# Score products of 128 weight columns, made as four of 32 columns, in a two-layer graph network

## The chip, the core and the metric

The kernel runs on one core of a Trainium2 chip. The metric is the device time of one execution in microseconds (us); lower is better. Three runs of the kernel before took 2897.25, 2900.75 and 2901.69 us; the median is 2900.75.

## What is computed

There are 64 graphs of 256 nodes with 256 features each, in fp32 throughout. Two layers follow each other. The first is a graph attention layer, applied twice, with a feed-forward part. The second is a relational attention layer, and the change lies there. Its core in the reference is:

```python
q = (src @ Wq + bq).reshape(Bb, Nn, h, dh).transpose(0, 2, 1, 3)
k = (src @ Wk + bk).reshape(Bb, Nn, h, dh).transpose(0, 2, 1, 3)
scores = jnp.einsum('bhid,bhjd->bhij', q, k) / np.sqrt(dh)
attn = jax.nn.softmax(scores, axis=-1)
out = jnp.zeros_like(q)
for r in range(Wv.shape[0]):
    v_r = (src @ Wv[r] + bv[r]).reshape(Bb, Nn, h, dh).transpose(0, 2, 1, 3)
    mask = (adj_matrix == r)[:, None]
    out = out + jnp.einsum('bhij,bhjd->bhid', attn * mask, v_r)
attn_out = out.transpose(0, 2, 1, 3).reshape(Bb, Nn, Dm) @ Wo + bo
x = _ln(src + attn_out, g1, beta1)
ff = jax.nn.gelu(x @ W1 + b1, approximate=False) @ W2 + b2
return _ln(x + ff, g2, beta2)
```

There are 8 heads of 32 features (`dh` = 32). The scores of one head are a product over only 32 features: 256 queries by 256 keys.

## The kernel before

The 64 graphs are worked on as 32 pairs. For each pair the kernel makes queries and keys transposed, that is, with the features on the partitions: in the tile `qk`, four heads of 32 features fill the 128 partitions, and two such halves (`c`) hold the eight heads.

TensorE multiplies a stationary operand, the weights (`lhsT`), by a streamed one (`rhs`). A product needs a weight load (PEld in the profile) and a matmul (PE). The array has 128 rows, over which a product sums, and 128 columns, one for each weight column and so for each partition of the output in PSUM. A product that uses only some rows or columns takes a tile of the array, and products in different tiles can be under way together. The profile gives the tile of a group as rows by columns: `128*32` or `32*128`.

Nearly every product of this kernel goes through `by_strips` (lines 160 to 163), which cuts 128 weight columns into four strips of 32, so four products with tiles of 128 rows by 32 columns stand side by side.

The score products do not. The function `scores(n)` (from line 1021) runs four times for each pair, for two graphs (`b`) and two halves of the heads (`c`). It takes four PSUM banks, one per head, and for two halves of the keys (`jc`) and four heads (`o`) it issues one matmul: the weights are 128 keys of one head (32 rows by 128 columns), the streamed operand is the 256 queries of this head. Head `o` has its 32 rows of the array to itself, so the four heads stand side by side in tiles of 32 rows by 128 columns. That is 8 products in one run of `scores`, and 4 x 32 = 128 runs of it, 1,024 products.

Behind it ScalarE takes the exponential of each bank (line 1038), VectorE masks it with the adjacency (L1042) and adds halves (L1046), and `products(n)` multiplies by the values (L1060) and sums the denominators (L1063), in tiles of 128 rows by 32 columns again. Between runs of `scores`, TensorE does other work in strips: feed-forward products of the same or the next layer (L163), projections, graph attention.

The order of all this is made by a planner in the kernel itself (`run`), when the program is built: each step names its costs, and `took(us)` moves the planned clock of TensorE forward. `scores` books `took(0.97)`. The order that results is fixed engine by engine in the program. The tensors have names in the profile: `ps` is any PSUM bank, `a` the exponentials, `m` the masked ones, `v` the values, `w_L_gnn_w_ff` and `w_L_gnn_W` the weights of the last feed-forward products, `ff` their other operand.

## Time and profile before

| what | value |
|---|---|
| the profiled execution | 2901.78 us |
| its span, first to last instruction | 2900.0 us |
| median of three runs | 2900.75 us |
| mean granted TensorE clock | 0.997 |
| TensorE (PE) busy | 2862.7 us |
| VectorE (DVE) busy | 2636.5 us |
| ScalarE (ACT) busy | 1910.2 us |
| weight loads (PEld) busy | 2038.1 us, beside PE |
| score products (L1029), matmul records | 2,048, busy 147.9 us |
| score products, weight-load records | 2,048, mean 184 ns |

A row of the profile's groups names the line of the kernel, the engine, the operation, the output and its inputs, the tile of the array as rows by columns, the shape of the streamed operand and the number of records. Busy time is the time in which at least one instruction of the group was under way, so the mean length of a matmul (some 400 ns) times its count is more than the busy time: four overlap. The ends of matmuls are modelled; their starts are measured. A waiting engine is idle, and the profile names what ended the wait. "issue" means that nothing which the profile shows was waited for.

In fp32 each matmul instruction shows as two weight loads and two matmuls, so the counts are twice those of the code.

### The profile page before, as it was taken

Reading aid. Unit: us, or ns where it says so; the run is one execution under the profiler, and the core shown is the slowest. Engines: PE = TensorE matmul, PEld = TensorE weight load, DVE = VectorE, ACT = ScalarE, POOL = GpSimd, SP = SyncE. Lnnn points to the kernel's source line nnn. Section 1 sums busy time; section 2 is a strip of 40 time slices with the busy share of each in tenths; the row PEclk is TensorE's granted clock in tenths of the full one; section 3 lists DMA queues with packets and bytes.
Section 4 is the critical chain, followed back from the end, with each engine's and each line's share of the span. In section 5 each row is a group of like instructions: output and inputs, shape, how many; then the busy total and the mean of one; then the engine's idle time right before and its main releaser. Section 6 shows DMA issues by size and latency. Waiting matters only on the chain.

```text
span 2900.0 us, 147819 instructions
## 1 busy us (share of the span) xinstructions
PE 2862.7 (99%) x66066; PEld 2038.1 (70%) x66066; DVE 2636.5 (91%) x5873; ACT 1910.2 (66%) x5171; POOL 285.3 (10%) x518
## 2 busy tenths in 40 slices
PE   8999999999999999999999999999999999999997
PEld 5766677877777676776777776776767776667676
DVE  7889999899999999999999999999999999999886
ACT  5656766656766667766567666677676676666765
POOL 0000010101010101101111100101011101010001
PEclk9999999999999999999999999999999999999999
DMA  6221212222222222222222222222222222221100
GB/s 206 74 68 61 78 61 82 74 79 79 65 68 76 83 80 63 78 72 78 80 76 65 69 76 83 75 75 76 68 78 83 73 69 67 77 75 51 54 3 25
DMA packets 207940, 211.85 MB, mean 73 GB/s; under 512 B 22593, under 2 KB 166337, under 8 KB 207041
## 3 DMA queue, kind: packets, MB, share of 16 engines
q1 hardware_dynamic: 206608, 201.79, 21.9%
q8 instruction: 520, 8.52, 1.2%
q14 instruction: 124, 1.01, 0.1%
q10 hardware_dynamic: 688, 0.53, 0.1%
HBM read 137.51 MB, written 64.73 MB: 70 GB/s over the span
## 4 chain that ended last, share of the span: by engine, by line
PE 93%; DVE 3%; DMA 2%; ACT 1%; issue 0%; SPq 0%; ACTq 0%; DVEq 0%; POOL 0%; POOLq 0%
PE ps L163 79%; PE ps L1060 7%; PE ps L1029 4%; PE ps L1063 2%; DMA yT<-home 0%; DVE ff L912 0%; DVE m L1042 0%; DVE x L739 0%; DMA home<-yb 0%; DMA b_ln<-in_ln 0%; DMA w_L_gnn_w_ff1p<-in_L_gnn_w_ff1pm 0%; DMA xw<-in_L_gnn_a1c 0%; DVE h L1046 0%; DVE x L736 0%; DVE ff L508 0%
## 5 line engine op out<-in xcount | busy, mean ns | idle before, releaser
L163 PE MATMUL ps<-w_L_gnn_w_ff,ff 128*32 128x128 f32 x14336 | 423.8, 273 | 2.5 <-DVE ff L508 1.6
L163 PE MATMUL ps<-w_L_gnn_W,ff 128*32 128x128 f32 x14336 | 424.2, 273 | 0.6 <-ACT a L1038 0.4
L163 PEld LDWEIGHTS ps<-w_L_gnn_w_ff,ff 128*32 128x32 f32 x14336 | 397.0, 110 | 35.2 <-issue 8.6
L163 PEld LDWEIGHTS ps<-w_L_gnn_W,ff 128*32 128x32 f32 x14336 | 393.5, 110 | 37.5 <-issue 15.9
L1038 ACT ACTIVATE a<-ps 128x512 f32<-128x512 f32 x512 | 264.3, 602 | 191.2 <-PE ps L1029 184.8
L912 DVE TENSOR_TENSOR ff<-ff 128x1024 f32<-128x1024 f32 x256 | 311.6, 1217 | 55.6 <-PE ps L163 39.7
L730 POOL TENSOR_SCALAR rstd<-squares 128x2 f32<-128x2 f32 x256 | 78.9, 308 | 2587.1 <-ACT unread L725 2586.6
L1042 DVE TENSOR_TENSOR m<-a,adj 128x1024 f32<-128x1024 f32 x256 | 308.1, 1217 | 3.3 <-ACT a L1038 2.9
L163 PE MATMUL ps<-yT,w_L_gnn_W1p 128*32 128x256 f32 x5120 | 305.8, 380 | 3.2 <-DMA yT<-home 3.1
L163 PE MATMUL ps<-yT,w_L_gnn_w_ff1p 128*32 128x256 f32 x5120 | 306.4, 379 | 0.0
L837 ACT ACTIVATE ff<-ps 128x512 f32<-128x512 f32 x384 | 221.1, 588 | 126.8 <-PE ps L163 126.1
L725 ACT ACTIVATE unread<-x,less 128x256 f32<-128x256 f32 x512 | 259.4, 507 | 68.3 <-DVE less L700 53.0
L508 DVE TENSOR_TENSOR ff<-ps,ff 128x512 f32<-128x512 f32 x384 | 255.9, 682 | 36.5 <-PE ps L163 23.3
L999 ACT ACTIVATE qk<-ps,bqk 128x256 f32<-128x256 f32 x256 | 109.7, 470 | 223.4 <-PE ps L163 223.1
L163 PE MATMUL ps<-xw,e 128*32 128x256 f32 (+1 forms) x4032 | 245.5, 383 | 1.3 <-ACT xw L630 1.3
L163 PEld LDWEIGHTS ps<-yT,w_L_gnn_W1p 128*32 128x32 f32 x5120 | 165.7, 110 | 106.0 <-ACT ff L837 6.8
L163 PEld LDWEIGHTS ps<-yT,w_L_gnn_w_ff1p 128*32 128x32 f32 x5120 | 168.7, 110 | 99.0 <-ACT unread L725 0.3
L736 DVE SCALAR_TENSOR_TENSOR x<-x,less,b_ln 128x256 f32<-128x256 f32 x512 | 227.5, 478 | 7.3 <-ACT unread L725 6.6
L739 DVE SCALAR_TENSOR_TENSOR x<-x,rstd,b_ln 128x256 f32<-128x256 f32 x512 | 229.4, 479 | 1.3 <-POOL rstd L731 1.3
L909 DVE TENSOR_TENSOR x<-ps,x 128x256 f32<-128x256 f32 (+1 forms) x384 | 193.9, 505 | 21.4 <-PE ps L163 16.2
L731 POOL TENSOR_TENSOR rstd<-rstd,mhalf 128x2 f32<-128x2 f32 x256 | 205.7, 803 | 21.3
L163 PEld LDWEIGHTS ps<-xw,e 128*32 128x32 f32 x4032 | 135.3, 111 | 84.8 <-issue 2.6
(141 smaller groups left out, 5015.6 us busy)
## 6 DMA issues: line engine op xcount, KB each, us to landing
home<-yb SPq DMA_DIRECT2D x182, 256.0 KB, 2.2
yT<-home SPq DMA_DIRECT2D x728, 64.0 KB, 2.1
rows<-row SPq DMA_DIRECT2D x60, 512.0 KB, 3.9
x<-in_x SPq DMA_DIRECT2D x32, 512.0 KB, 3.8
out<-x SPq DMA_DIRECT2D x64, 256.0 KB, 3.1
input<-in_xT SPq DMA_DIRECT2D x30, 512.0 KB, 3.9
input<-in_adjT SPq DMA_DIRECT2D x29, 512.0 KB, 4.0
m<-in_adjT SPq DMA_DIRECT2D x3, 512.0 KB, 8.8
```

Of the source, the lines that this page charges most:

```text
L163: nc.tensor.matmul(to[at:at + DH], lhsT=lhsT[:, at:at + DH], rhs=rhs, **flags)
L508: nc.vector.tensor_tensor(self.target(*where), self.bank["z"], self.target(*where), ALU.add)
L725: nc.scalar.activation(unread, rows[j], AF.Square, bias=of["less"][:, j:j + 1], accum_out=squares[:, j:j + 1])
L731: nc.gpsimd.tensor_tensor(rstd, rstd, mhalf[:, :2], ALU.pow)
L736: nc.vector.scalar_tensor_tensor(rows[j], rows[j], of["less"][:, j:j + 1], g, op0=ALU.add, op1=ALU.mult)
L739: nc.vector.scalar_tensor_tensor(rows[j], rows[j], rstd[:, j:j + 1], beta, op0=ALU.mult, op1=ALU.add)
L837: return put("scalar", 0.5, lambda: nc.scalar.activation(target(c, h), of, AF.Copy), event, rank=rank_of["copies"])
L909: return put("vector", us, lambda: nc.vector.tensor_tensor(to, of, to, ALU.add), *events, rank=rank_of["last"], frees=frees)
L912: return put("vector", 1.14, lambda: nc.vector.tensor_tensor(to, a, b, op), *events, rank=rank_of["sums"])
L1038: nc.scalar.activation(a[n][q][:, k], ps[2 * q + k], AF.Exp)
L1042: nc.vector.tensor_tensor(m[n][q], a[n][q], adj, ALU.mult)
L1060: nc.tensor.matmul(po[o * DH:(o + 1) * DH, :N], lhsT=v[:, b, jc, at:at + DH], rhs=e[o // 2][:, o % 2, jc * N:(jc + 1) * N], start=r == jc ...
```

## The change

The inner product of `scores` is made in four parts. Each part takes 32 of the 128 weight columns (keys) and writes 32 of the 128 partitions of the same bank. The streamed operand, the 256 queries of the head, is the same for the four parts. The tile becomes 32 rows by 32 columns. A run of `scores` issues 32 products where it issued 8; the planner still books 0.97 us for it.

```diff
     HQ = P // DH
+    PART = 32
     SCALE = 1.0 / math.sqrt(DH)
...
                 at = b * N + jc * P
                 for o in range(HQ):
                     rows = slice(o * DH, (o + 1) * DH)
-                    nc.tensor.matmul(ps[o][:, jc * N:(jc + 1) * N], lhsT=qk[rows, 1, c, at:at + P],
-                                     rhs=qk[rows, 0, c, b * N:(b + 1) * N], start=True, stop=True)
+                    for part in range(0, P, PART):
+                        nc.tensor.matmul(ps[o][part:part + PART, jc * N:(jc + 1) * N],
+                                         lhsT=qk[rows, 1, c, at + part:at + part + PART],
+                                         rhs=qk[rows, 0, c, b * N:(b + 1) * N], start=True, stop=True)
             there = took(0.97)
```

## The prediction

> **What bounds the kernel now.** I read the page first: busy shares, then the chain that ended last.

> ```profile
> span 2900.0 us, 147819 instructions
> PE 2862.7 (99%) x66066; PEld 2038.1 (70%) x66066; DVE 2636.5 (91%) x5873; ACT 1910.2 (66%) x5171; POOL 285.3 (10%) x518
> ...
> PE 93%; DVE 3%; DMA 2%; ACT 1%; issue 0%; SPq 0%; ACTq 0%; DVEq 0%; POOL 0%; POOLq 0%
> PE ps L163 79%; PE ps L1060 7%; PE ps L1029 4%; PE ps L1063 2%; DMA yT<-home 0%; DVE ff L912 0%; DVE m L1042 0%; DVE x L739 0%; DMA home<-yb 0%; DMA b_ln<-in_ln 0%; DMA w_L_gnn_w_ff1p<-in_L_gnn_w_ff1pm 0%; DMA xw<-in_L_gnn_a1c 0%; DVE h L1046 0%; DVE x L736 0%; DVE ff L508 0%
> ```

> TensorE is the bound from end to end, so what the score products (L1029) take on it counts nearly one for one. A busy PE need not be an efficient one, so next the groups of instructions by shape. The columns after the bar are the busy time of the group and the mean ns of one record.

> ```profile
> L163 PE MATMUL ps<-w_L_gnn_w_ff,ff 128*32 128x128 f32 x14336 | 423.8, 273 | 2.5 <-DVE ff L508 1.6 <-DVE ff L912 0.9
> ...
> L1029 PE MATMUL ps<-qk 32*128 32x256 f32 x2048 | 147.9, 400 | 0.0
> L1060 PE MATMUL ps<-m,v 128*32 128x256 f32 x2048 | 135.4, 380 | 0.0
> ```

> A matmul instruction leaves two records in fp32: 1,024 score products show as 2,048. Scores cost 147.9/2048 = 72 ns a record; the weighted products of L1060, which stream the same 256 columns through tiles of 128 rows by 32 columns, 66 ns. Then the one line, and one block of it (16 records) with its neighbours in the timeline.

> ```profile
> L1029 PEld LDWEIGHTS ps<-qk x2048: 181/184/185, 153.2 to 2827.2; 32*128 32x128 f32 x187
> L1029 PE MATMUL ps<-qk x2048: 374/374/478, 153.2 to 2827.4; 32*128 32x256 f32 x187
> ```

> ```profile
> 402.58 1.93 PE L163 MATMUL ps<-w_L_gnn_W,ff 128*32 128x128 f32 x64
> 404.44 1.15 PE L1029 MATMUL ps<-qk 32*128 32x256 f32 x16
> 405.52 1.95 PE L163 MATMUL ps<-w_L_gnn_W,ff 128*32 128x128 f32 x64
> 407.29 1.05 PE L163 MATMUL ps<-yT,w_L_gnn_W1p 128*32 128x256 f32 x16
> 408.15 1.05 PE L1060 MATMUL ps<-a,v 128*32 128x256 f32 x16
> 409.02 1.05 PE L1060 MATMUL ps<-m,v 128*32 128x256 f32 x16
> ```

> From start to start, 16 records of strips of 256 columns take 0.87 us (408.15 to 409.02), which is 54 ns each or four side by side every 0.216 us. The score block takes 1.08 us (404.44 to 405.52): 0.21 more inside itself. The 64 records ahead of it take 1.86, the same 64 behind it 1.77: another 0.09 to 0.11 at the entry, where the shape of the tiles changes. Where the 0.21 lies is seen when another block, at 153.17, is cut into short stretches (of each engine, the x counts the instructions that touch the stretch):

> ```profile
> 153.16:153.19 0.03, 0.03 (x4) 0.03 (x4) 1.00 0.00 0
> 153.19:153.27 0.07, 0.07 (x4) 0.07 (x4) 1.00 0.00 0
> 153.27:153.30 0.03, 0.03 (x4) 0.03 (x8) 1.00 0.00 0
> 153.30:153.49 0.18, 0.18 (x4) 0.18 (x8) 1.00 0.00 0
> 153.49:153.51 0.03, 0.03 (x8) 0.02 (x4) 1.00 0.00 0
> ...
> 153.91:153.94 0.03, 0.03 (x8) 0.00 (x0) 1.00 0.00 0
> 153.94:154.24 0.29, 0.29 (x8) 0.00 (x0) 1.00 0.21 83
> ```

> Four heads start within 0.03 us, a second wave of four at 153.49, the last at 153.91, the next shape at 154.24. So: first wave 0.32, two waves of 0.21, last 0.33, where a hidden wave is 0.216. The first is about 0.10 longer (its weights load in the open: the longest record is 478 against 374 ns, 104 more), the last about 0.11 [...]. Entry, first wave and exit add up to some 0.32 us a block; there are 128 blocks (four for each of 32 pairs), 41 us in all. That is all the change can touch.

> [...] The trace shows the four heads within 0.03 us, some 7 ns apart, for a tile that has two loads and two multiplies. [...]

> **The change, part by part.** The order of instructions is the same on every engine; on PE each row of 8 score products becomes 32, because the planner still books 0.97 us for the block. No wait, buffer or DMA is added; the waits for the four banks stay on the first product of each head.

> 1. Array work: the same. Eight products of 32 rows by 128 columns are half an array-load twice over; 32 of 32 by 32 are 16 tiles, each used twice. If the 16 run together, each tile streams 2 products x 2 passes = 4 waves of 0.216, as before. Cost 0.
> 2. Removed: most of the open first load. With 32 columns the same start in strips shows 24 ns (the shape of 128x128 goes from 273 to 297-298 in its first wave), against 104. Gain 0.08 us a block.
> 3. Added: the sixteenth tile starts later than the fourth. At 6.7 ns a tile, 15 x 6.7 = 0.10 against 3 x 6.7 = 0.02[...]. Loss 0.08 us.
> 4. Drains at entry and exit: still a change of shape, 128 rows against 32. Cost 0. If the smaller tile empties faster [...], gain up to 0.21 us; I take 0.
> 5. Issue: 48 more records a block, each a load and a multiply. No row prices this. From below: 0[...]. From above: at the start of the program, in products of four streamed columns, 8 matmuls touch the first stretch below and 20 the next, so 12 begin within 0.18 us, 15 ns each; with no queue at all the 64th comes at 0.96 us, where the last of the block starts at 0.77 now. Loss at most 0.19 us. I take 0[...].

> ```profile
> 12.30:12.36 0.06, 0.06 (x8) 0.05 (x4) 0.00 (x0) 0.00 (x0) 1.00 1.19 359
> 12.36:12.54 0.18, 0.18 (x20) 0.18 (x12) 0.00 (x0) 0.00 (x0) 1.00 1.10 347
> ```

> 6. Weight loads of tiles on the same rows: strips show four columns loading together. If with row tiling they took turns, [...] (loss of the 0.08 of step 2). I take 0.
> 7. Who reads: ACT's exponentials (L1038) waited 184.8 us for these products, but ACT is 66% busy and off the chain; a shift under 0.1 us is hidden there. A shift of 1 us would hold up PE anyway, through PE's own time.

> Sum of steps 2 and 3: 128 x (-0.08 + 0.08) = 0. On the profiled execution (2901.78 us, of which 2900.0 are span and 1.8 around it) that is 2901.8; the median of the runs shown is 1.0 lower, so I forecast 2901. A difference under 0.2%, 6 us, can't be told from none.

> **The rivals.**
> - *Four lanes, not sixteen* (slower). The trace shows four tiles at once, never more: four row groups or four column groups. If what lets a second tile pass the waiting second pass of a first is a lane per row group or per column group, the four parts of a head (or the four heads of a part) stand in one line: the second pass of a part runs beside the first pass of the next only. A lane then holds 8 products: 9 waves, not 4, so +5 x 0.216 = 1.08 us, less 0.08: +1.0 us x 128 = +128, 3029 us. It decides as soon as the lane is a group and not a tile. For it: no sight of sixteen in fp32. Against: [...] that strips share rows and heads share columns, yet both run four wide.
> - *Issue or loads show* (slower). Steps 5 and 6 at their ends: +0.08 to +0.27 us, +10 to +35: 2911 to 2936. For it: four times the instructions in the same time. Against: the four-column stretch.
> - *Faster*: the drain shrinks with the tile, or first passes are issued before the waiting second ones, halving the skew (-0.05). From -0.05 to -0.29 us (0.08 of load plus 0.21 of drain): -6 to -37, likely near the small end, 2890 us. [...] Against: the drain at the entry is that of the strips, and stays.

> **How the numbers follow.** No change (within 6 us) 0.34; issue or loads 0.24; four lanes 0.15; faster 0.27. The likeliest is no change, 2901, with its own range 2895 to 2907. The range over cases reaches from 2876 (most of faster) to 2936 (issue and loads at their ends) and leaves out the four lanes and the far end of faster, under 0.2 together. Faster by over 0.2%: 0.27; within: 0.34; slower: 0.24 + 0.15 = 0.39.

> **What would show it.** Right: 8,192 score records (4 x 2,048) whose starts come sixteen within about 0.1 us; weight loads near 110 ns; the block still near 1.08 us and 16 or more multiplies touching one short stretch. Step 2 wrong: the longest score matmul stays 100 ns above the median. Step 3 wrong: sixteen starts in much less or more than 0.1. Step 5: gaps between starts with no tile busy, or "issue" ahead of the loads of the next shape. Lanes: never more than four starts per 0.216 us, the block near 2 us, and L1029's share of the chain near doubled. The forecast falls if the block's length moves by more than 45 ns, which is 6 us over 128 blocks.

## The result, and the profile after

The changed kernel took 2952.6 us (median of six runs, 2948.21 to 2954.33) against 2901.22 before (six runs beside them). The ratio is 1.0175, with a 95% interval of 1.0164 to 1.0186: slower by 51 us. The forecast was 2901, with a range up to 2936.

The profiled execution took 2948.21 us, the lowest of the six, with a span of 2946.4: 46.4 more than the span before. TensorE is the bound as before. First the page's span, busy shares and chain by line of the changed kernel, then its groups by shape (busy us and mean ns after the bar), then the one line (durations as min/median/max ns).

```profile
span 2946.4 us, 160107 instructions
...
PE 2911.1 (99%) x72210; PEld 2111.9 (72%) x72210; DVE 2640.9 (90%) x5873; ACT 1909.5 (65%) x5171; POOL 290.6 (10%) x518
...
PE ps L164 78%; PE ps L1063 7%; PE ps L1031 6%; PE ps L1066 2%; DMA x<-in_x 1%; DMA home<-yb 1%; DMA yT<-home 0%; SPq L784 0%; DVE ff L913 0%; PE ps L804 0%; DVE x L740 0%; DVE x L737 0%; ACT unread L726 0%; PE ps L1179 0%; DVE yb L773 0%
```

```profile
L1031 PE MATMUL ps<-qk 32*32 32x256 f32 x8192 | 195.3, 385 | 0.9 <-DVE x L910 0.9
```

```profile
L1031 PEld LDWEIGHTS ps<-qk x8192: 101/104/106, 153.1 to 2875.4; 32*32 32x32 f32 x200
L1031 PE MATMUL ps<-qk x8192: 371/374/399, 153.1 to 2875.7; 32*32 32x256 f32 x200
```

The scores' share of the chain went from 4% to 6%, their busy time from 147.9 to 195.3 us: 47.4 more, about as much as the span grew. VectorE and ScalarE are busy about as long as before (2640.9 and 1909.5 us, against 2636.5 and 1910.2). The open load did shrink: the longest matmul stands 25 ns above the median (399 against 374), where it was 104 before. A weight load takes 104 ns, against 184 before.

The timeline around the same block as before gives its length:

```profile
405.47 1.93 PE L164 MATMUL ps<-w_L_gnn_W,ff 128*32 128x128 f32 x64
407.33 1.61 PE L1031 MATMUL ps<-qk 32*32 32x256 f32 x64
408.88 1.95 PE L164 MATMUL ps<-w_L_gnn_W,ff 128*32 128x128 f32 x64
```

The entry is as before (1.86 us for the 64 records ahead). This block is 1.55 us from its start to the next. Most are shorter: the median of the 128 is 1.425 us, against 1.076 before. The one at 1737.51 is such a block, and its stretches show what happened. The columns are PE and PEld (busy, and the instructions that touch the stretch), then the granted clock and the DMA traffic. Times in the text below count from the start of the block.

```profile
1737.50:1737.60 0.10, 0.10 (x14) 0.10 (x25) 1.00 0.84 328
1737.60:1737.63 0.03, 0.03 (x16) 0.03 (x30) 1.00 1.22 478
...
1737.74:1737.87 0.13, 0.13 (x32) 0.11 (x2) 1.00 0.93 347
1737.87:1737.95 0.08, 0.08 (x32) 0.00 (x0) 1.00 0.98 384
1737.95:1738.06 0.11, 0.11 (x25) 0.10 (x1) 1.00 1.10 428
1738.07:1738.14 0.07, 0.07 (x17) 0.00 (x0) 1.00 0.75 293
1738.14:1738.42 0.28, 0.28 (x31) 0.27 (x30) 1.00 0.13 44
```

Sixteen matmuls begin in the first 0.12 us and are under way together (x16): sixteen tiles do run side by side. By 0.36 us all 32 of the first half of the keys have begun (x32). (A fp32 product leaves two matmul records here, 8,192 for 4,096 products; the text calls them its first and second pass.) Then one product of the second half gets in: its second load is the one near 0.46 us, and x17 later is the sixteen second passes and this product. From 0.57 to 0.63 us no load is under way at all. The 17th product's load began with its tile's second pass (0.241 and 0.240); on the other fifteen tiles the second passes have begun by 0.36, and no load has followed. Only from 0.65 us on do the others follow, and slowly: the next fifteen are spread over 0.23 us, 16.7 ns each, where the first fourteen came 6.7 ns apart.

The starts of the single records add up the lost time of this block. The 18th product begins at 0.650 us. It could have begun at 0.462, one step of 6.7 ns after the 17th (0.456): 0.188 lost. The sixteenth tile's second product comes 0.233 after that, at 16.7 ns a product, and not 0.093 at 6.7: 0.140. Its load is open again: 0.022. The sum is 0.350. The last start of a block moved from 0.771 before to 1.121 us, as much. Times 128 blocks this is 45 us, of the 46.4 in the span.

### The profile page after: what moved, and what is told of

Read it like the earlier page. It is cut to its first block, busy times and chain, and to the rows that moved or that the text cites. A ratio compares the mean times of both kernels' runs of the same rounds, so it can differ in the third digit from the quotient of the medians.

```text
span 2946.4 us, 160107 instructions
## 1 busy us (share of the span) xinstructions
PE 2911.1 (99%) x72210; PEld 2111.9 (72%) x72210; DVE 2640.9 (90%) x5873; ACT 1909.5 (65%) x5171; POOL 290.6 (10%) x518
## 4 chain that ended last, share of the span: by engine, by line
PE 94%; DMA 2%; DVE 2%; ACT 1%; issue 1%; SPq 0%; DVEq 0%; POOL 0%; POOLq 0%; ACTq 0%
PE ps L164 78%; PE ps L1063 7%; PE ps L1031 6%; PE ps L1066 2%; DMA x<-in_x 1%; DMA home<-yb 1%; DMA yT<-home 0%; SPq L784 0%; DVE ff L913 0%; PE ps L804 0%; DVE x L740 0%; DVE x L737 0%; ACT unread L726 0%; PE ps L1179 0%; DVE yb L773 0%
## 5 line engine op out<-in xcount | busy, mean ns | idle before, releaser
L731 POOL TENSOR_SCALAR rstd<-squares 128x2 f32<-128x2 f32 x256 | 86.6, 338 | 2628.1 <-ACT unread L726 2627.5
L164 PEld LDWEIGHTS ps<-yT,w_L_gnn_w_ff1p 128*32 128x32 f32 x5120 | 180.9, 110 | 90.0 <-ACT unread L726 0.4
L164 PEld LDWEIGHTS ps<-xw,e 128*32 128x32 f32 x4032 | 144.3, 111 | 77.1 <-issue 3.3
```

The source lines that it names most:

```text
L164: nc.tensor.matmul(to[at:at + DH], lhsT=lhsT[:, at:at + DH], rhs=rhs, **flags)
```

## Experiments

### Two parts of 64 columns

```diff
-    PART = 32
+    PART = 64
```

> The four parts of 32 columns become two of 64 (tiles of 32 rows by 64 columns, 16 products a block). Theory W, a window in the matrix engine: it holds some 64 to 68 instructions that are issued and not finished, let go in order; a product in fp32 is 4 of them, so the 18th product of the changed block waits for the first tile's second pass (0.46 to 0.65 us after the block's start). With 16 products the block is 64 instructions and fits: no gap, an open load of about 0.05 us, eight tiles 0.05 us apart from first to last, block about 1.05 us, 2896 to 2902 us. Theory R, a rule of the tile: a second product in a tile of less than 128 columns holds back all others until it is under way. Then a gap of about 0.19 us stays, block about 1.25 us, about 2922 us.

Measured: 2900.22 us, ratio to the kernel before 0.9999 (0.9991 to 1.0007). The line and one block in the timeline:

```profile
L1031 PE MATMUL ps<-qk x4096: 371/374/426, 152.3 to 2827.2; 32*64 32x256 f32 x196
```

```profile
1710.10 1.12 PE L1031 MATMUL ps<-qk 32*64 32x256 f32 x32
1711.14 1.08 PE L164 MATMUL ps<-w_L_gnn_w_ff,ff 128*32 128x128 f32 x32
```

The block takes 1.04 to 1.05 us, as W said, with no gap. The open load is 52 ns (426 against 374) with 64 columns, between 104 with 128 and 25 with 32: here it goes by the columns. Eight tiles are used twice here, too, so that a tile is used a second time is not what costs. Against before the block is 0.027 us shorter, which would be 3.5 us of 2900; the timed runs don't show it.

### The parts outside the heads

```diff
-                for o in range(HQ):
-                    rows = slice(o * DH, (o + 1) * DH)
-                    for part in range(0, P, PART):
+                for part in range(0, P, PART):
+                    for o in range(HQ):
+                        rows = slice(o * DH, (o + 1) * DH)
...
```

> The same 32 products of 32 by 32, with the loop over the parts outside that over the heads, so neighbours in the order stand in different row groups and banks. W: only the count matters, 17 products ahead of the gap, block 1.42 us, within 4 us of the changed kernel (2952). A rule of row groups (R, or weights of one row group loading in turn): the gap moves or goes, block other than 1.42 by more than 0.1 us.

Measured: 2952.1 us in one run, block 1.42 to 1.43 us (1736.35 to 1737.78 in the timeline). In its records the 18th product begins at 0.649 us, one first product of the second half ahead of it. Neighbours in other row groups and banks changed nothing here (0.649 against 0.650), so a shared row group is not the cause.

### Two heads first

```diff
-            for jc in range(2):
-                at = b * N + jc * P
-                for o in range(HQ):
+            for two in range(0, HQ, 2):
+                for jc in range(2):
+                    at = b * N + jc * P
+                    for o in range(two, two + 2):
...
```

> Heads 0 and 1 make both halves of the keys before heads 2 and 3 begin: eight tiles used twice are the first 64 instructions, and the next products go to eight tiles that nothing has used in this block. W: these idle tiles wait too, all but one of them until about 0.65 us; then four waves follow, block about 1.7 us, about 2990 us. R: a fresh tile isn't held back, it starts within about 0.15 us of the block's start or as soon as the second product of the first tile has begun at 0.46; the gap stands at the second product of the first tile, the 9th product, not at the 18th.

Measured: 2986.2 us in one run, block 1.75 us. The matmuls of one block, which begins at 1758.155, by stretches (PE only):

```profile
1758.15:1758.20 0.05, 0.04 (x7) 1.00 0.00 0
1758.40:1758.46 0.06, 0.06 (x16) 1.00 0.00 0
1758.66:1758.78 0.12, 0.12 (x17) 1.00 1.12 444
1758.79:1758.92 0.13, 0.13 (x29) 1.00 0.86 347
```

At 0.51 to 0.62 us (third line) seventeen matmuls are under way: eight second passes, the eight tiles' second products, and one from a fresh tile. Seven more tiles have had no work in this block and get none until 0.65. So the wait belongs to no tile: R falls. It is the 18th product that waits, in a used tile in the changed kernel and in a fresh one here.

The records of this run tell two more things of the wait. By their modelled ends, sixteen loads and eight first passes had finished by 0.45 us, and still nothing behind the 17th product came in until 0.65, when the oldest product was done: by these ends the order counts, not only the number. And the 17th product, alone in a fresh tile and with its weights loaded, begins at 0.426 us in all 128 blocks, 28 ns after the modelled end of the first product's first pass (0.398). Its first matmul is the 66th record and that pass the second. So if this start was a wait for that pass, the estimate of W comes down to 64 records; with 65 it would not have had to wait for it.

### Three heads first

```diff
-            for jc in range(2):
-                at = b * N + jc * P
-                for o in range(HQ):
+            for heads in (range(3), range(3, HQ)):
+                for jc in range(2):
+                    at = b * N + jc * P
+                    for o in heads:
...
```

> Heads 0 to 2 make both halves of the keys, then head 3 both. Twelve tiles are used once by the first 48 instructions. W: 17 products still start ahead of the gap, so five second products (not one) start near 0.46 to 0.49 us, the gap ends near 0.65; block about 1.8 us, about 3000 us. R: one second product ahead of the gap, as in the changed kernel.

Measured: 2986.3 us in one run, block 1.79 us. The block begins at 1756.62:

```profile
1756.61:1756.70 0.09, 0.08 (x12) 1.00 0.00 0
1756.86:1756.94 0.08, 0.08 (x24) 1.00 0.44 179
1757.11:1757.22 0.11, 0.11 (x17) 1.00 0.95 372
1757.26:1757.45 0.19, 0.19 (x28) 1.00 0.96 377
```

Twelve first products, then at 0.49 to 0.60 us x17: the twelve second passes and five second products. That is 12 + 5 = 17 products ahead of the gap, as W counts them, and the records show the sixth at 0.650. In these runs the count of products is the same, and the place is not.

### Half the stream

```diff
-                for o in range(HQ):
-                    ...
+                for i in range(0, N, P):
+                    for o in range(HQ):
+                        ...
```

The streamed operand of a product is the 128 queries from `i` on, so 64 half-long products do the same work.

> Each of the 32 products of 32 by 32 is cut once more along the streamed side, 128 queries at a time: 64 products a block, half as long, the same work in the array. Theory W (64 instructions issued and not finished, released in order when the first tile's second pass is done): that pass starts near 0.13 us and ends near 0.40, so the gap behind the 17th product ends near 0.43 us, not 0.65. After it products come 16.7 ns apart, as in the changed kernel behind its gap; last start near 1.3 to 1.4 us, block about 1.6 us, about 2975 us. Theory F (the feed of instructions pauses for a time of its own after such a burst, whatever finishes): the gap still ends near 0.65 us, and returns for each 16 products, block above 2 us, above 3020 us.

Measured: 3122.2 us in one run. One block, from 1839.46 to 1841.29, is 1.83 us. The stretches (PE, then PEld):

```profile
1839.73:1839.77 0.04, 0.04 (x32) 0.00 (x0) 0.00 (x0) 0.00 (x0) 1.00 1.30 512
1839.80:1839.88 0.08, 0.08 (x25) 0.08 (x1) 0.00 (x0) 0.00 (x0) 1.00 1.03 410
1839.88:1839.98 0.10, 0.10 (x19) 0.09 (x10) 0.00 (x0) 0.00 (x0) 1.00 0.58 216
```

The gap is there (no loads at 0.27 to 0.31 us, one after), and it ends by 0.43 us: at 0.43 to 0.52 ten loads touch the stretch. So its end follows the first tile's second pass, which is over sooner with a stream half as long, and not a time of its own. That is W, and F falls as the cause of this gap. The starts, which are measured, say it without the modelled ends: from the start of the first product's second pass to the load of the 18th product it is 405 to 406 ns in the changed kernel and in the three runs before this one, and 298 here. The 108 less is half a stream of 0.216 us. The 17th product, too, whose tile is free from about 0.24 us on, begins at 0.318: 26 ns after the modelled end of the first product's first pass (0.292).

The time of the whole, though, missed by 147 us, and a gap that returns and a time above 3020 us are what F expected. I had the typical block 0.2 too short (1.83 against about 1.6): by W, too, the gap should return for every sixteen products, with the slow pace behind it. And the waits of PE show something else:

```profile
PE ps L164 <- issue: 44.5, 67, 1.9
PE ps L1032 <- issue: 29.4, 36, 2.6
```

With 256 instructions a block TensorE idles 74 us for no releaser, up to 2.6 us at once. In the changed kernel the same waits sum to 2.8 us, so they are not the cause of its gap. Their times go with the packets of the instruction queue: of the 108 idle stretches of TensorE over 0.2 us in this trace (behind the first 40 us), 87, with 68 of their 86 us, end 1.3 to 1.7 us after a packet of the instruction queue has landed. Packets are 4.9 us apart, so chance would give one in twelve; in the kernel before it is none of 15. That the feed of instructions runs dry there is the author's reading of these times; no run tested it by a change.

The account of the 221 us is rough. Some half of the blocks are near 1.83 us (0.755 more than before, which would be 97 us for all 128), the others are longer; all together the blocks grew by 137 us, waits included, so some 84 lie outside them.

### Half the stream, parts of 64 columns

```diff
-    PART = 32
+    PART = 64
```

This edit is made on the kernel of the run above.

> Two parts of 64 columns, each product cut in two along the streamed side (128 queries): 32 products a block, 128 instructions, as many as in the changed kernel, but a tile is used four times for half as long, so eight tiles have few instructions unfinished at once. Theory W (64 instructions issued and not finished): the first tile's second pass, begun near 0.16 us, is done near 0.45 us, before the 18th product could start at about 0.5 us; no gap. 8 products per 0.22 us is 27 ns each, slower than the 16.7 ns refill pace. Block about 1.05 to 1.10 us, 2895 to 2906 us. Theory C (the count of instructions in a block costs, whatever is unfinished: 128 of them at the pace of issue): block about 1.4 us, about 2945 to 2955 us.

Measured: 2928.0 us, ratio 1.0095 (1.0078 to 1.0112). Its block in the timeline:

```profile
2085.29 1.21 PE L1032 MATMUL ps<-qk 32*64 32x128 f32 x64
2086.43 1.95 PE L164 MATMUL ps<-w_L_gnn_w_ff,ff 128*32 128x128 f32 x64
```

The block has as many instructions as the changed kernel's and takes 1.14 us, not 1.4: the count in itself (C) does not make the 0.35. But it is not free either. The wait is here as worked out: the load of the 18th product begins at 0.459 us, 299 ns after the first product's second pass began (298 in the run above, with the same stream), and its matmul at 0.494, as soon as its tile is free. What I had wrong is the pace behind it. Loads come 16.7 ns apart from 0.459 on, but the eight tiles come free 6.7 ns apart, not evenly at 27 ns; the 18th to 21st products still begin on time, and from the 22nd on each is late. The block is 0.06 us longer than before, or 8 us over 128 blocks; the other 20 of the 28 us lie outside the typical block. Waits for "issue" sum to 9.7 us, and 22 of 37 idle stretches, with 14 of their 24 us, end 1.3 to 1.7 us after an instruction packet; the rest was not traced to a cause.

## Why the prediction was wrong

- **What bounds the kernel**: right. All of the loss is in the score blocks on TensorE, one for one.
- **Step 1, sixteen tiles side by side**: right for the first sixteen products (sixteen starts in 0.12 us), wrong for the block. Four waves as before need the second product of each tile to begin as soon as its tile is free, and that did not hold.
- **Step 2, the open load**: right: 25 ns, where 24 was taken.
- **Step 3, the skew**: 0.10 to 0.12 us against 0.10, nearly right.
- **Step 4, drains** (the time at a change of shape): right to take no change. The 64 records ahead of the block take 1.86 us as before, and the next shape begins 0.30 us after the last start, as before (1.121 to 1.425, against 0.771 to 1.076).
- **Step 6, loads on the same rows**: right to take 0. In the trace before, four strip loads are under way together (x4 at 5.15 to 5.25 us). Here 25 loads touch the first 0.1 us, the first fourteen products began 6.7 ns apart, and the open load is 25 ns.
- **Step 5, issue: the step that failed.** It took 0, with an end of 0.19. It measured 0.35: 0.188 of waiting for the 18th product, 0.140 of slow pace behind it and 0.022 of an open load. Two things were missing. The 48 more records were priced only as work to be issued; that what is under way counts too, until the oldest is finished, was not thought of, and the trace before shows no sign of it. And behind the wait the rest came at 16.7 ns a product, where the first fourteen had come at 6.7. The bound of 0.19 did not catch this, and for another reason than its pace. Its 15 ns were for a record (a load and a multiply), where the trace shows 16.7 for a product of two such records, some 8 ns each; and they were read in a stretch where four tiles restart every 53 ns, which is the pace of the tiles. Set beside a start at 0, 8 ns a record would have cost nothing (64 x 8 is 0.51 us, and the last starts at 0.77 before); the cost comes because issue stops and goes on only at 0.65. The sign named for this step, starts apart with no tile busy, did not show either: the tiles were busy with second passes.
- **"All the change can touch"**: the 41 us of entry, first wave and exit bound what could be saved. The loss lies in the waves between, which were counted as hidden.
- **The rivals**: four lanes did not occur. "Issue or loads show" named the right side and, with issue, the right step, but not what holds it; its end of 2936 was too low, by the same term. "Faster" did not occur: the gain of the load (0.08) was the skew's loss, and the drain did not shrink.

What stays open: whether loads count in W as matmuls do. Every matmul of these kernels has its load (72,210 records of each in the changed kernel), so an estimate of 64 instructions and one of 32 matmuls fit all runs alike. That the slow pace behind the wait is the pace of issue was not shown.

## What to carry to other kernels

In this kernel side-by-side tiles cost instructions in flight. Where tiles are used more than once, one round over them is tiles x the records of a product (two loads and two matmuls in fp32 here). Eight tiles (32 records a round) took 1.05 and 1.14 us for blocks of 64 and 128 records; sixteen tiles (64 a round, all that W has room for by the estimate above) took 1.42 and 1.83 for 128 and 256 (the second of each pair with half the stream). Two parts of 64 columns halved the open load and lost nothing, four parts lost 0.35 us a block. So in a like kernel count a round before cutting the weights further, and try the coarser cut beside the finer one. A bound on issue is to be laid from the moment at which issue can go on (0.65 us here), not from the start of the block.

## What the runs showed of the hardware

- Sixteen 32 by 32 tiles in fp32 did run at once (x16 in one stretch of the changed kernel). The first fourteen products of the typical block began 6.7 ns apart; behind the wait they came 16.7 ns apart (4.2 ns a record).
- With two heads first, seven tiles without work in the block got none until 0.65 us, about when the oldest product, in another tile, was done.
- The load of the 18th fp32 product began 405 to 406 ns after the first one's second pass with 256 streamed columns, and 298 to 299 with 128, in the typical blocks of six kernels.
- The open load at the change of shape was 104, 52 and 25 ns with 128, 64 and 32 columns.
- Cutting the streamed operand in two, with the same work in the array, brought idle time without a releaser: 74 us with 64 products a block. Of the idle stretches over 0.2 us, 87 of 108 ended 1.3 to 1.7 us after an instruction packet had landed.
